# A third Strassen level over pairs of steps, in three of seven rounds of a float32 linear layer

## The chip, the cores and the metric

The kernel runs on one core of a Trainium2 chip. The metric is the device time of one execution in microseconds (us), as the median of several runs. TensorE (PE) multiplies; VectorE (DVE) adds products from the accumulation banks (PSUM) into partial sums in SBUF; GpSimd (POOL) makes sums and differences of operands in SBUF; SyncE (SP) issues most of the loads and stores.

## The reference

All arrays are float32. The part that matters here is the first feed-forward layer, a linear map over the last axis of length 2048, applied to `x` of shape (32, 128, 2048):

```
out = einsum('bsd,od->bso', x, W) + bias                  # W is 2048 x 2048
upd = sum over e of coeffs[e]*scales[e] * (x A_e^T) Bf_e^T  # 16 updates of rank 16
x   = x + out + upd    # after a mixing of the 128 rows, per batch entry
```

In the kernel the low-rank updates are first added to `W`, so that one product with a 2048 x 2048 matrix is left. The mixing of the rows (`agg_w`, 128 x 128 for each batch entry) commutes with that product and is done after it. Then follow a grouped convolution with 9 taps along the length and a second feed-forward layer with 16 heads (128 to 512 to 128, with a gelu), whose rows are permuted.

## The kernel before

The linear layer is done with Strassen's scheme in Winograd's form, on two levels.

The **outer level** splits `x` and the weights into two by two blocks and gives seven products, the *rounds*, in the order `ROUNDS = ("P1", "P2", "P6", "P7", "P5", "P3", "P4")` (line 48). The two row blocks are the two halves of a group of four batch entries. A round needs one sum or difference of weight blocks and, for each of eight groups `g`, one sum or difference of x blocks. A *step* is one round and one group, `(r, g)`; there are 56, numbered `i`.

The **inner level** is in `multiply` (line 322). For a step it makes seven products, again called P1 to P7, each of four matmuls over chunks `kc` of 128 of the contraction, with an x tile of 128x128 as the stationary operand and a weight tile of 128x512 as the moving one. Three PSUM banks (`px`, `py`, `pz`) hold running sums of these products, and after every product `add` has DVE add the bank into one 128x512 part of a partial sum in SBUF. The partial sums of a round are loaded from DRAM (`olds_load`, line 908), added to, and stored again under a new name (`ADDED`, line 312; `part_store`, line 268). Round P5 has two partials per step, the others have one.

The operands are made on POOL. `x_combine` (line 288) makes the block of x of the outer level (`pieces`, line 271, 4 operations for each sum of two tiles) and then the four inner sums `s` (lines 302 to 305). `inner_weights` (line 238) makes the inner weights `t1`, `t2`, `t4` (12 operations) and one difference in place (4 operations), once per round, in the last step of the round before (in round P1, in its seventh step). `outer_weights` (line 369) loads the weight blocks of the next round during steps g = 2 to 5 of this one, one chunk `kc` in a step, and its `combine` adds them in the step after: P6 has three source tiles per chunk, P7 and P5 two, P4 two, P3 one.

Order: the program is scheduled by hand (`tc.manual_schedule()`), so that each engine and each queue works in the order of the code. In step `i` the code issues `x_combine` for step `i+1`, the x loads for step `i+2`, the load of the partial of step `i+1`, at the last step of a round `inner_weights` for the next, then the combination of a weight chunk and the load of the next one, then the matmuls of step `i`, and at their end the store of the partial, which stands on SP's queue ahead of the loads of the next step.

Most tiles are slots of one pool `big` of 24 (`SLOTS = 24`, line 35), each 128 x 2048 float32. A new tile takes the place of one whose last reader or writer is done; where no slot is free, the instruction that writes the new tile first waits, and with it all behind it on its queue.

Three other things use slots or engines in these rounds. `mixed_kernel` (line 402) puts small DVE operations between the products of the first six steps of a round (`between`) and holds one slot. The generator `small` (line 727) goes on by one piece after each step; in round P2 it makes the transformed convolution weights in two slots, `tw` and `t1` (lines 832 to 855). The convolution in the last part of the kernel has the only other matmuls with 256 columns (`conv_product`, line 539).

Of the kernel before, what the change touches and what calls it, by code (L numbers as in the profile page):

```python
# [11 lines left out]
ALU = mybir.AluOpType  # L12
# [4 lines left out]
P = 128  # L17
# [10 lines left out]
NQ = QW // 2  # L28
# [19 lines left out]
ROUNDS = ("P1", "P2", "P6", "P7", "P5", "P3", "P4")  # L48


@with_exitstack
def adaln_ffn_kernel(
    ctx: ExitStack,
# [15 lines left out]
    nc = tc.nc  # L69
# [8 lines left out]
    def slot(name, shape=(P, L)):  # L78
        return big.tile(list(shape), FP, name=name, tag="s")


    def bank():
        return banks.pop(0)

    def done(*ps):
        banks.extend(ps)

    def scratch(name, shape=(P, L)):
        return dram.tile(list(shape), FP, name=name, tag=name)
# [178 lines left out]
    def part_store(n, g, t, eng=nc.gpsimd):  # L268
        eng.dma_start(part_d[n, g], t.rearrange("p k s c -> p (k s c)"))

    def pieces(out, a, b, op):

        for i in range(2):
            for j in range(2):
                nc.gpsimd.tensor_tensor(out[:, i, j], a[:, i, j], b[:, i, j], op)  # L275
# [12 lines left out]
    def x_combine(r, g, ts):  # L288

        a = ts[0]  # L290
        tt = nc.gpsimd.tensor_tensor
        if r == "P6":

            b, a, c = ts
            pieces(b, b, a, ALU.add)
            pieces(a, b, c, ALU.subtract)
            part_store("s2", g, a)
        if r in ("P7", "P5", "P3"):
            pieces(a, a, ts[1], ALU.add if r == "P5" else ALU.subtract)
        s = slot(f"s_{r}{g}", (P, 4, QW))  # L300
        a11, a12, a21, a22 = a[:, 0, 0], a[:, 1, 0], a[:, 0, 1], a[:, 1, 1]
        tt(s[:, 0], a21, a22, ALU.add)  # L302
        tt(s[:, 1], s[:, 0], a11, ALU.subtract)
        tt(s[:, 2], a11, a21, ALU.subtract)
        tt(s[:, 3], a12, s[:, 1], ALU.subtract)
        return {
            "P1": a11, "P2": a12, "P3": s[:, 3], "P4": a22,
            "P5": s[:, 0], "P6": s[:, 1], "P7": s[:, 2],
        }


    ADDED = {
        "P1": [(None, "p1")],
        "P2": [("p1", "c00")],
        "P6": [("p1", "u1")],
        "P7": [("u1", "u2")],
        "P5": [("u1", "u3"), ("u2", "c11")],
        "P4": [("u2", "c10")],
        "P3": [("u3", "c01")],
    }  # L320

    def multiply(r, g, lhs, rhs, olds, between):
        px, py, pz = bank(), bank(), bank()
        accs = olds if olds[0] is not None else [slot(f"m_{r}{g}", (P, 2, 2, QW))]
        fresh = set()

        def add(si, oi, ps):
            for acc in accs:
                to = acc[:, si, oi]
                if olds[0] is not None or (si, oi) in fresh:  # L330
                    nc.vector.tensor_tensor(to, ps, to, ALU.add)  # L331
                else:
                    nc.scalar.copy(to, ps)
            fresh.add((si, oi))

        def product(k, ps, first, last):
            for kc in range(4):
                nc.tensor.matmul(  # L338
                    ps, lhsT=lhs[k][:, bass.ts(kc, P)], rhs=rhs[k][kc],
                    start=first and kc == 0, stop=last and kc == 3, skip_group_check=True,  # L340
                )

        product("P1", px, True, False)
        add(0, 0, px)
        between(0)
        product("P2", pz, True, True)
        add(0, 0, pz)
        done(pz)
        between(1)
        product("P6", px, False, False)  # L350
        add(0, 1, px)
        between(2)
        product("P5", py, True, False)
        add(1, 1, py)
        between(3)
        product("P7", px, False, False)
        add(1, 1, px)
        between(4)
        product("P3", py, False, True)
        add(0, 1, py)  # L360
        done(py)
        between(5)
        product("P4", px, False, True)
        add(1, 0, px)
        done(px)
        for (_, new), acc in zip(ADDED[r], accs):
            part_store(new, g, acc, nc.sync)

    def outer_weights(r, kc):

# [129 lines left out]
    def conv_inputs(c, i, part):  # L500
# [27 lines left out]
        else:  # L528
# [3 lines left out]
            w0, w5 = v0[:, :, 1:NM], v5[:, :, 0 : NM - 1]  # L532
            stt(w0, d[3][:, :, 0 : NM - 1], 4.0, w0, ALU.mult, ALU.add)
            stt(w5, d[0][:, :, 1:NM], 0.25, w5, ALU.mult, ALU.add)

    def halves(t):
        return [t[:, r * NQ : (r + 1) * NQ] for r in range(2)]

    def conv_product(ps, k, i, v, first, last):

# [321 lines left out]
    steps = [(r, g) for r in ROUNDS for g in range(NG)]  # L862
# [19 lines left out]
    lhs, sa, tb = {}, {}, {}  # L882
    sa[0] = a_combine(0, nc.gpsimd.tensor_tensor)
    first = [wt.pop(k) for k in blocks[0:4]]
# [15 lines left out]
    rhs = inner_weights("P1", first, make_first)  # L900
    a_load(1, 0, 4)
    unsummed, unsummed_first = [], list(first)
    olds = {}
    chain = small()
    nxt, waiting, ts = {}, {}, {}
# [6 lines left out]
    for i, (r, g) in enumerate(steps):  # L912
        ri = i // NG
        last_round = ri + 1 == len(ROUNDS)
        if i + 1 < len(steps):
            if i + 1 not in xs:
                xs[i + 1] = x_loads(*steps[i + 1])
            if not last_round:
                lhs[i + 1] = x_combine(*steps[i + 1], xs.pop(i + 1))
        if i + 2 < len(steps) and ri > 0 and not last_round:  # L920
            xs[i + 2] = x_loads(*steps[i + 2])
        if i == 0:
            olds_load(0)
        if i + 1 < len(steps) and not last_round:
            olds_load(i + 1)
        if g == NG - (1 if ri else 2) and ri < len(ROUNDS) - 1:
            nxt = inner_weights(ROUNDS[ri + 1], [nxt[kc] for kc in range(4)])

        if ri == 0:
            ks = blocks[4 + 2 * g : 6 + 2 * g]  # L930
            if ks:
                two = [wt.pop(k) for k in ks]
                w_make_two(ks, two, sa[ks[0][0]], tb[ks[0][1]])
                made.extend(ks)
                if g == 1:
                    a_scale(1, 0, 4)
                    sa[1] = a_combine(1, nc.gpsimd.tensor_tensor)
                if g == 3:
                    part, tb[0] = b_combine(0, nc.gpsimd.tensor_tensor)
                    for _ in range(4):  # L940
                        part()
                for k, t in zip(ks, two):
                    unsummed.append((k[1], t))
                    if k[:2] == (1, 0):
                        nxt[k[2]] = t
        elif ri + 1 < len(ROUNDS):
            for k, combine in waiting.items():
                nxt[k] = combine()
            waiting = {}
            if 2 <= g < 6:  # L950
                waiting[g - 2] = outer_weights(ROUNDS[ri + 1], g - 2)

        if last_round and g == 0:
            late_loads()
        if last_round and g == 2:

            late["te"] = mix.rearrange("p (k r) c -> p k r c", k=2)
            nc.sync.dma_start(mix.rearrange("p k c -> p (k c)"), te_d)
        k0 = 3 * (g - NG)
        if last_round:  # L960
            stage(k0, stage_first)

        def between(j):
            b = (ri - 1) * (NG - 2) + g
            if ri > 0 and g < NG - 2 and b < B and j < KEXP // 2:
                mixed_kernel(b, (2 * j, 2 * j + 1))
            if ri == 0 and j == 2:
                for k in blocks[6 + 2 * g : 8 + 2 * g]:
                    wt[k] = w_load(*k)
            if ri == 0 and j in (1, 3) and unsummed:  # L970
                row_sums(*unsummed.pop())
            if ri == 0 and j == 5 and unsummed_first:
                t = unsummed_first.pop(0)
                tt = nc.vector.tensor_tensor
                tt(wsum[:, 0, 0], wsum[:, 0, 0], t[:, 0, 0], ALU.add)
                tt(wsum[:, 0], wsum[:, 0], t[:, 1], ALU.add)
            if last_round:
                if j == 3 and i + 1 < len(steps):
                    lhs[i + 1] = x_combine(*steps[i + 1], xs.pop(i + 1))
                    olds_load(i + 1)  # L980
                if j in (2, 4):
                    stage(k0 + j // 2, stage_first)
                if j % 2:
                    stage_third(k0 + j // 2)
                else:
                    stage(k0 + j // 2, stage_second)

        multiply(r, g, lhs.pop(i), rhs, olds.pop(i), between)
        next(chain, None)
        if last_round and g >= 6:  # L990
            pair(g - 6)
        if last_round and g == 7:
            rings()
            gather_two(0)
        if g == NG - 1 and ri + 1 < len(ROUNDS):
            rhs = nxt
            nxt = {}

    before = None
    for k, (g, h) in enumerate(heads):  # L1000
# [5 lines left out]
        t = ts.pop(k)  # L1006
# [75 lines left out]
```

## Time and profile before

| | |
|---|---|
| median of 3 runs | 2629.42 us (2627.97 to 2631.45) |
| the profiled execution | 2628.45 us |
| its span, first to last instruction | 2626.7 us |
| granted TensorE clock, mean | 0.999 |
| PE busy | 2611.2 us, 99% |
| POOL busy | 1234.8 us, 47% |
| DVE busy | 1349.3 us, 51% |
| HBM traffic | 372.45 MB read, 200.84 MB written |

In a list of groups a row gives the line, engine, operation and tile names, the count, the busy time and the mean duration of one. In a timeline a row gives the start, the time from the start of the first to the end of the last, what it is, and in brackets how long the engine was idle before it and for whom it waited. In a table of stretches each row gives the stretch, its length, the busy time of PE, PEld (the load of stationary operands), DVE, ACT and POOL with the count of instructions, the granted clock, the share of DMA and the rate in GB/s. A float32 matmul appears as two instructions of PE, called passes here, each with a load of the stationary operand before it. PE's rows overlap their successors, so passes are compared from start to start.

### The profile page before, as it was taken

What the parts mean: (1) busy time and instruction counts of PE and PEld (TensorE: products, weight loads), DVE (VectorE), ACT (ScalarE), POOL (GpSimd) and SP (SyncE); (2) the same over time, 40 slices, a digit from 0 to 9 for tenths busy, and PEclk for the clock granted to TensorE, in tenths of its full rate; (3) what the DMA queues carried; (4) which work ended last, traced back from release to release, by engine and by line L of the source; (5) the groups of instructions that cost most, each with busy time, mean ns of one, the idle gap of its engine ahead of it and who ended that gap; (6) DMA issues with size and microseconds to landing.
All of it is one profiled execution on the core that took longest, in us unless ns stands there. A gap on an engine that the chain in (4) does not pass through costs nothing.

```text
span 2626.7 us, 20239 instructions
## 1 busy us (share of the span) xinstructions
PE 2611.2 (99%) x6468; PEld 1228.9 (47%) x6468; DVE 1349.3 (51%) x2178; ACT 532.9 (20%) x1099; POOL 1234.8 (47%) x1014
## 2 busy tenths in 40 slices
PE   9999999999999999999999999999999999999998
PEld 4444444444444444444444445555444555555543
DVE  5554234354233454433366666666666666666610
ACT  0000000000000000000011144444444444444432
POOL 7320636888756644756342334434443344344222
PEclk9999999999999999999999999999999999999999
DMA  7542358688466577565668798777778777777532
GB/s 304 223 162 109 130 222 310 270 338 351 159 241 256 221 285 294 224 243 202 224 221 256 223 319 284 234 228 220 225 249 250 243 225 222 238 250 232 166 121 88
DMA packets 183833, 608.20 MB, mean 232 GB/s; under 512 B 17200, under 2 KB 88368, under 8 KB 139440
## 3 DMA queue, kind: packets, MB, share of 16 engines
q1 hardware_dynamic: 149936, 473.74, 50.8%
q0 software_dynamic: 32992, 132.14, 14.9%
q10 hardware_dynamic: 800, 1.03, 0.1%
q8 instruction: 52, 0.85, 0.1%
q14 instruction: 53, 0.43, 0.1%
HBM read 372.45 MB, written 200.84 MB: 218 GB/s over the span
## 4 chain that ended last, share of the span: by engine, by line
PE 98%; DVE 1%; DMA 1%; issue 0%; SPq 0%; POOLq 0%; ACT 0%; DVEq 0%; ACTq 0%
PE bank L338 51%; PE bank L687 16%; PE bank L698 16%; PE bank L543 6%; PE bank L448 4%; PE bank L216 3%; PE bank L173 1%; DMA ws<-in_ffw 0%; DVE vb L523 0%; DVE va L522 0%; DMA bf_sb<-in_BfT 0%; DVE vb L521 0%; DVE va L524 0%; DMA out<-t,orow 0%; DVE aggb L782 0%
## 5 line engine op out<-in xcount | busy, mean ns | idle before, releaser
L687 PE MATMUL bank<-t,ws 128*128 128x512 f32 x1024 | 460.4, 592 | 0.8 <-DMA ws<-in_ffw 0.8
L698 PE MATMUL bank<-gl,ws 128*128 128x512 f32 x1024 | 460.2, 592 | 0.0
L705 POOL DMA_INDIRECT out<-t,orow x128 | 153.5, 1199 | 532.2 <-DVE t L703 451.6
L331 DVE TENSOR_TENSOR u<-bank,u 128x512 f32<-128x512 f32 x280 | 187.9, 688 | 416.5 <-PE bank L338 409.4
L690 ACT ACTIVATE gl<-bank 128x512 f32<-128x512 f32 x512 | 306.2, 598 | 446.2 <-PE bank L687 443.2
L338 PE MATMUL bank<-P_t,s_P 128*128 128x512 f32 x896 | 393.7, 592 | 0.0
L698 PEld LDWEIGHTS bank<-gl,ws 128*128 128x128 f32 x1024 | 194.6, 190 | 233.0 <-issue 231.0
L687 PEld LDWEIGHTS bank<-t,ws 128*128 128x128 f32 x1024 | 194.5, 190 | 227.7 <-issue 223.6
L433 POOL TENSOR_TENSOR x<-x,fb 128x512 f32<-128x512 f32 x128 | 178.0, 1418 | 228.1 <-DMA x<-in_x 201.0
L338 PE MATMUL bank<-wo_P,s_P 128*128 128x512 f32 x640 | 281.6, 592 | 0.9 <-DVE u L331 0.9
L338 PE MATMUL bank<-wo_P,xt 128*128 128x512 f32 x640 | 281.5, 592 | 0.0
L338 PEld LDWEIGHTS bank<-P_t,s_P 128*128 128x128 f32 x896 | 170.2, 190 | 213.4 <-issue 211.2
L703 DVE TENSOR_TENSOR t<-bank,t 128x512 f32<-128x512 f32 x128 | 88.5, 691 | 316.1 <-PE bank L698 315.9
L439 ACT ACTIVATE bank<-w,aggb 128x512 f32<-128x512 f32 x128 | 80.8, 683 | 793.6 <-DMA w<-w_d 776.3
L275 POOL TENSOR_TENSOR xt<-xt,xt 128x512 f32<-128x512 f32 x128 | 160.0, 1283 | 150.3 <-DMA xt<-in_xT 135.5
L338 PE MATMUL bank<-P_t,xt 128*128 128x512 f32 x448 | 201.4, 592 | 0.0
L331 DVE TENSOR_TENSOR p<-bank,p 128x512 f32<-128x512 f32 x112 | 77.5, 692 | 228.5 <-PE bank L338 225.1
L338 PEld LDWEIGHTS bank<-wo_P,s_P 128*128 128x128 f32 x640 | 121.5, 190 | 153.0 <-issue 149.7
L338 PEld LDWEIGHTS bank<-wo_P,xt 128*128 128x128 f32 x640 | 121.6, 190 | 152.2 <-issue 150.9
L302 POOL TENSOR_TENSOR s_P<-xt 128x512 f32<-128x512 f32 x56 | 72.3, 1291 | 254.8 <-DMA xt<-in_xT 198.0
L412 DVE SCALAR_TENSOR_TENSOR ags<-mix,att_bc,ags 128x128 f32<-128x128 f32 x224 | 162.9, 727 | 4.5
L671 POOL DMA_INDIRECT t<-hx_d,row x128 | 131.9, 1030 | 50.6 <-issue 26.0
(141 smaller groups left out, 2648.9 us busy)
## 6 DMA issues: line engine op xcount, KB each, us to landing
xt<-in_xT SPq DMA_DIRECT2D x88, 1024.0 KB, 9.0
u<-u_d SPq DMA_DIRECT2D x40, 1024.0 KB, 11.0
wo_P<-wb_d SPq DMA_DIRECT2D x36, 1024.0 KB, 14.4
u<-c_d SPq DMA_DIRECT2D x64, 512.0 KB, 7.3
x<-in_x SPq DMA_DIRECT2D x32, 1024.0 KB, 8.0
xg<-x SPq DMA_DIRECT2D x256, 128.0 KB, 5.1
hx_d<-x1t SPq DMA_DIRECT2D x32, 1024.0 KB, 6.0
hx_d<-ht SPq DMA_DIRECT2D x32, 1024.0 KB, 7.1
```

Source lines behind the costliest of these rows:

```text
L275: nc.gpsimd.tensor_tensor(out[:, i, j], a[:, i, j], b[:, i, j], op)
L331: nc.vector.tensor_tensor(to, ps, to, ALU.add)
L338: nc.tensor.matmul(ps, lhsT=lhs[k][:, bass.ts(kc, P)], rhs=rhs[k][kc], start=first and kc == 0, stop=last and kc == 3, skip_group_check=True,)
L412: nc.vector.scalar_tensor_tensor(ag, mix[:, k], att, ag, ALU.mult, ALU.add)
L433: nc.gpsimd.tensor_tensor(xt[:, f], xt[:, f], late["fb"][:, f], ALU.add)
L448: nc.tensor.matmul(pm, lhsT=ag, rhs=u[:, f], start=False, stop=True, skip_group_check=True)
L543: nc.tensor.matmul(out, lhsT=w[:, 2 * i + r], rhs=rhs, start=first and r == 0, stop=last and r == 1, skip_group_check=True,)
L671: nc.gpsimd.indirect_dma_start(out=t.rearrange("p k t -> p (k t)"), out_offset=None, in_=hx_d[g].rearrange("l k t -> l (k t)"), in_offset= ...
L687: nc.tensor.matmul(pu, lhsT=w[:, m * P : (m + 1) * P], rhs=t[:, 0], start=True, stop=True)
L690: nc.scalar.activation(gl[m], pu, AF.Gelu)
L698: nc.tensor.matmul(pd, lhsT=w[:, (MC + m) * P : (MC + m + 1) * P], rhs=gl[m], start=(m == 0), stop=(m == MC - 1),)
L705: nc.gpsimd.indirect_dma_start(out=out, out_offset=bass.IndirectOffsetOnAxis(ap=orow[:, g, h : h + 1], axis=0), in_=t[:, 1], in_offset=None,)
```

## The change

In rounds P2, P7 and P3 the inner products P2 and P4 of two neighbouring steps (an even `g` and the next) are taken together. The two steps give two blocks of rows, the contraction is cut into two halves of 256 and the columns into two halves of 256, and each of the two inner products is made by seven products of a third Strassen level, *quarters*. A quarter is made for both inner products at once, in the two halves of one PSUM bank: for each, two matmuls of 128x128 by 128x256.

- `multiply_third` takes the place of `multiply` in these rounds. In an even step it makes five products (P1, P5, P6, P3, P7). In the odd step it makes these five and the seven quarters, in three more banks (`qx`, `qy`, `qz`), and DVE adds each quarter's bank into one half of a partial of one of the two steps. The bank after product P7 is added into two parts of the partial, where P4's was added into the second before. Both partials are stored at the end of the odd step.
- `third_inputs` makes four sums of x blocks per pair on POOL, into one slot, right after the `x_combine` of the odd step. `third_weights` makes eight differences for each of the two inner products on POOL (16 operations of 128x256, two slots), right after `inner_weights`, so in the last step of the round before (for P2, in the seventh step of P1).
- The x tile of the even step and its partial stay in their slots until the odd step uses them.

```diff
+THIRD = ("P2", "P7", "P3")
...
+    def third_weights(name, rhs):
+        quarters, tt = [], nc.gpsimd.tensor_tensor
+        for i, k in enumerate(("P2", "P4")):
+            t = slot(f"{name}_q{i}", (P, 4, 2, NQ))
...
+            for kc in range(2):
+                (r11, r12), (r21, r22) = (halves(rhs[k][2 * h + kc]) for h in range(2))
+                tt(t[:, 0, kc], r12, r11, ALU.subtract)
+                tt(t[:, 1, kc], r22, t[:, 0, kc], ALU.subtract)
+                tt(t[:, 2, kc], r22, r12, ALU.subtract)
+                tt(t[:, 3, kc], r21, t[:, 1, kc], ALU.subtract)
...
+    def third_inputs(i):
+        (x11, x12), (x21, x22) = (
+            [xa[n][:, 1, :, h * NQ : (h + 1) * NQ] for h in range(2)] for n in (i, i + 1)
+        )
...
+        t = slot(f"sq_{i}", (P, 4, 2, NQ))
+        tt(t[:, 0], x21, x22, ALU.add)
+        tt(t[:, 1], t[:, 0], x11, ALU.subtract)
+        tt(t[:, 2], x11, x21, ALU.subtract)
+        tt(t[:, 3], x12, t[:, 1], ALU.subtract)
...
+    def multiply_third(r, g, lhs, rhs, olds, between, quarters, sq):
+        px, py = bank(), bank()
+        if sq:
+            qx, qy, qz = bank(), bank(), bank()
+            both = [held.pop(), olds]
...
+        def quarter(k, ps, first, last, *to):
+            if not sq:
+                return
+            for i, out in enumerate(halves(ps)):
+                for kc in range(2):
+                    nc.tensor.matmul(
+                        out, lhsT=sq[k][:, i, bass.ts(kc, P)], rhs=quarters[i][k][kc],
...
+            for b, h in to:
+                for acc in both[b]:
+                    part = acc[:, :, 0, h * NQ : (h + 1) * NQ]
+                    nc.vector.tensor_tensor(
+                        part, ps.rearrange("p (s n) -> p s n", s=2), part, ALU.add
+                    )
+        product("P1", px, True, False)
+        add(0, 0, px)
+        between(0)
+        quarter("P1", qx if sq else None, True, False, (0, 0))
+        quarter("P2", qz if sq else None, True, True, (0, 0))
...
+        product("P5", py, True, False)
+        add(1, 1, py)
+        between(1)
+        quarter("P6", qx if sq else None, False, False, (0, 1))
+        quarter("P5", qy if sq else None, True, False, (1, 1))
+        product("P6", px, False, False)
+        add(0, 1, px)
+        between(2)
+        quarter("P7", qx if sq else None, False, False, (1, 1))
+        quarter("P3", qy if sq else None, False, True, (0, 1))
...
+        product("P3", py, False, True)
+        add(0, 1, py)
...
+        quarter("P4", qx if sq else None, False, True, (1, 0))
...
+        product("P7", px, False, True)
+        add(1, 1, px)
+        add(1, 0, px)
...
+        if not sq:
+            held.append(olds)
+            return
+        for b, accs in enumerate(both):
+            for (_, new), acc in zip(ADDED[r], accs):
+                part_store(new, g - 1 + b, acc, nc.sync)
...
@@ the loop over the steps
                 lhs[i + 1] = x_combine(*steps[i + 1], xs.pop(i + 1))
+                if r in THIRD and g % 2 == 0:
+                    sq = third_inputs(i)
...
             nxt = inner_weights(ROUNDS[ri + 1], [nxt[kc] for kc in range(4)])
+            if ROUNDS[ri + 1] in THIRD:
+                nxt["quarters"] = third_weights(ROUNDS[ri + 1], nxt)
...
-        multiply(r, g, lhs.pop(i), rhs, olds.pop(i), between)
+        if r in THIRD:
+            multiply_third(
+                r, g, lhs.pop(i), rhs, olds.pop(i), between, rhs["quarters"], sq if g % 2 else None
+            )
+        else:
+            multiply(r, g, lhs.pop(i), rhs, olds.pop(i), between)
```

More of the change, by code (lines that the diff above doesn't have):

```diff
@@ L86, in done, with halves @@
         banks.extend(ps)
+    def halves(t):
+        return [t[:, r * NQ : (r + 1) * NQ] for r in range(2)]
     def scratch(name, shape=(P, L)):
@@ L299, in x_combine @@
             pieces(a, a, ts[1], ALU.add if r == "P5" else ALU.subtract)
+        xa[steps.index((r, g))] = a
         s = slot(f"s_{r}{g}", (P, 4, QW))
@@ L309, in x_combine @@
         }
+    xa = {}
     ADDED = {
@@ L367, in multiply @@
             part_store(new, g, acc, nc.sync)
+    def third_weights(name, rhs):
+        quarters, tt = [], nc.gpsimd.tensor_tensor
+        for i, k in enumerate(("P2", "P4")):
+            t = slot(f"{name}_q{i}", (P, 4, 2, NQ))
+            q = {"P1": [], "P2": [], "P3": [], "P4": [], "P5": [], "P6": [], "P7": []}
+            for kc in range(2):
[4 more added lines that the diff above has]
+                tt(t[:, 3, kc], r21, t[:, 1, kc], ALU.subtract)
+                for n, r in zip(q, (r11, r21, r22, t[:, 3, kc], t[:, 0, kc], t[:, 1, kc], t[:, 2, kc])):
+                    q[n].append(r)
+            quarters.append(q)
+        return quarters
@@ new lines, in third_inputs @@
+    def third_inputs(i):
+        (x11, x12), (x21, x22) = (
+            [xa[n][:, 1, :, h * NQ : (h + 1) * NQ] for h in range(2)] for n in (i, i + 1)
+        )
+        tt = nc.gpsimd.tensor_tensor
+        t = slot(f"sq_{i}", (P, 4, 2, NQ))
[3 more added lines that the diff above has]
+        tt(t[:, 3], x12, t[:, 1], ALU.subtract)
+        return {
+            "P1": x11, "P2": x12, "P3": t[:, 3], "P4": x22,
+            "P5": t[:, 0], "P6": t[:, 1], "P7": t[:, 2],
+        }
@@ new lines, in multiply_third, with add, product @@
+    def multiply_third(r, g, lhs, rhs, olds, between, quarters, sq):
[3 more added lines that the diff above has]
+            both = [held.pop(), olds]
+        def add(si, oi, ps):
+            for acc in olds:
+                nc.vector.tensor_tensor(acc[:, si, oi], ps, acc[:, si, oi], ALU.add)
+        def product(k, ps, first, last):
+            for kc in range(4):
+                nc.tensor.matmul(
+                    ps, lhsT=lhs[k][:, bass.ts(kc, P)], rhs=rhs[k][kc],
+                    start=first and kc == 0, stop=last and kc == 3, skip_group_check=True,
+                )
[4 more added lines that the diff above has]
+                for kc in range(2):
+                    nc.tensor.matmul(
+                        out, lhsT=sq[k][:, i, bass.ts(kc, P)], rhs=quarters[i][k][kc],
+                        start=first and i == 0 and kc == 0, stop=last and i == 1 and kc == 1,
+                        skip_group_check=True,
+                    )
[4 more added lines that the diff above has]
+                        part, ps.rearrange("p (s n) -> p s n", s=2), part, ALU.add
+                    )
+        product("P1", px, True, False)
[3 more added lines that the diff above has]
+        quarter("P2", qz if sq else None, True, True, (0, 0))
+        if sq:
+            done(qz)
+        product("P5", py, True, False)
[8 more added lines that the diff above has]
+        quarter("P3", qy if sq else None, False, True, (0, 1))
+        if sq:
+            done(qy)
+        product("P3", py, False, True)
+        add(0, 1, py)
+        done(py)
+        between(3)
+        quarter("P4", qx if sq else None, False, True, (1, 0))
+        if sq:
+            done(qx)
+        product("P7", px, False, True)
+        add(1, 1, px)
+        add(1, 0, px)
+        done(px)
+        between(4)
+        between(5)
+        if not sq:
[4 more added lines that the diff above has]
+                part_store(new, g - 1 + b, acc, nc.sync)
@@ L369, in outer_weights @@
+    held = []
     def outer_weights(r, kc):
@@ L534, in conv_inputs @@
             stt(w5, d[0][:, :, 1:NM], 0.25, w5, ALU.mult, ALU.add)
-    def halves(t):
-        return [t[:, r * NQ : (r + 1) * NQ] for r in range(2)]
     def conv_product(ps, k, i, v, first, last):
@@ L986, in between @@
                     stage(k0 + j // 2, stage_second)
-        multiply(r, g, lhs.pop(i), rhs, olds.pop(i), between)
+        if r in THIRD:
+            multiply_third(
+                r, g, lhs.pop(i), rhs, olds.pop(i), between, rhs["quarters"], sq if g % 2 else None
+            )
+        else:
+            multiply(r, g, lhs.pop(i), rhs, olds.pop(i), between)
+        xa.pop(i - 1, None)
         next(chain, None)
```

## The prediction

> **What bounds the kernel now.** I read the page first: busy times, slices, chain. TensorE is busy in every slice at full granted clock, and the chain that ended last is 98% PE.
>
> ```profile
> PE 2611.2 (99%) x6468; PEld 1228.9 (47%) x6468; DVE 1349.3 (51%) x2178; ACT 532.9 (20%) x1099; POOL 1234.8 (47%) x1014
> ...
> PEclk9999999999999999999999999999999999999999
> ...
> PE 98%; DVE 1%; DMA 1%; issue 0%; SPq 0%; POOLq 0%; ACT 0%; DVEq 0%; ACTq 0%
> ```
>
> So only removed matmul time helps, and only while PE keeps being fed. Next, the seven rounds as stretches (P2 begins at 306.5 us, each step lasts 24.03, the chain's "24.03 PE bank L338 x56").[...]
>
> ```profile
> 306.50:498.70 192.20, 192.20 (x449) 85.05 (x449) 73.18 (x109) 2.37 (x4) 106.38 (x87) 1.00 0.67 256
> 498.70:691.00 192.30, 192.30 (x450) 85.15 (x449) 83.80 (x106) 0.63 (x1) 172.66 (x143) 1.00 0.76 298
> 691.00:883.20 192.20, 192.20 (x450) 85.05 (x449) 68.47 (x104) 0.00 (x0) 114.58 (x94) 1.00 0.59 229
> ```
>
> P2, P6, P7 (P3 is like P7): PE never idles, POOL has 70 to 86 of 192 us left in the rounds that change. Third, the timeline of PE around a convolution, the only 256-column matmuls, and of POOL and SP at the end of round P2:
>
> ```profile
> 1341.46 1.88 PE L338 MATMUL bank<-wo_P,s_P 128*128 128x512 f32 x4
> 1343.18 1.89 PE L543 MATMUL bank<-va,tw_l 128*128 128x256 f32 x8
> 1344.91 3.60 PE L338 MATMUL bank<-P_t,xt 128*128 128x512 f32 x8
> ```
> ```profile
> 480.89 1.27 POOL L245 TENSOR_TENSOR P_t<-wo_P 128x512 f32<-128x512 f32 x1 [1.77 <-issue]
> 485.16 1.27 POOL L246 TENSOR_TENSOR P_t<-wo_P,P_t 128x512 f32<-128x512 f32 x1 [2.99 <-PE bank L338]
> 488.59 1.27 POOL L247 TENSOR_TENSOR P_t<-wo_P,P_t 128x512 f32<-128x512 f32 x1 [2.17 <-PE bank L338]
> ```
> ```profile
> 451.44 0.32 SPq L269 DMA_DIRECT2D c_d<-p  x1
> 451.86 4.78 SPq L260 DMA_DIRECT2D xt<-in_xT  x3
> 456.73 0.38 SPq L265 DMA_DIRECT2D p<-p_d  x1
> ```
>
> [...]Four passes of 512 columns start 1.72 us apart (0.429 each), eight of 256 take 1.73 (0.216 each). The other two say that the 24 slots of SBUF are already used up at the end of P2: POOL waits for PE to finish with the old weights before t2 and t4 of P6 have a place (474.7+10.3 and +13.7 us are the ends of that round's last P6 and P5 products), and three loads take 4.78 us to issue because the third waits for a freed source tile. Counting live tiles through the code gives exactly 24 at that point, so the count can be trusted.
>
> **The change, part by part.**
>
> *PE.* Per pair of steps the P2 and P4 products go: 2 steps x 2 products x 4 chunks x 2 passes = 32 passes x 0.429 = 13.73 us. They are replaced by 7 quarters x 4 matmuls x 2 passes = 56 passes x 0.216 = 12.10. Saved: 1.63 a pair; three rounds of four pairs make 12 pairs, **19.5 us**. All of it lies on the path. An even step becomes 5 x 3.43 = 17.2 us long, an odd one 17.2+12.1 = 29.3.
>
> A rule speaks against this. The Trainium skill, "TensorE: Matmul & The Clock Gate", section "The mechanism", says that a weight load overlaps a running matmul only when it goes to another row group. All matmuls here use all 128 rows, and a load lasts 190 ns in the groups; by the rule a pair would go from 32 x (0.429+0.19) = 19.8 to 56 x (0.216+0.19) = 22.7, which is 35 us slower over 12 pairs. The rows above show 0.216 from start to start with a load before each pass, so the loads are hidden, and I take the rows. The cover is thin: 190 of 216 ns.
>
> *DVE.* Additions into one partial: 14 a pair before; now 6 in each step and 7 after quarters, 19. 5 x 0.69 = 3.5 us a pair, 41 in all, beside PE: DVE has 68 to 73 us busy of 192 here and needs 19 x 0.69 + 16 x 0.74 (mixed_kernel) = 25 of 46 us a pair. Between a quarter and the next use of its bank lie at least 5 us of PE. Nothing, while the partials are there in time.
>
> *POOL.* third_inputs: 4 operations of the size of s (1.27 us), 5.1 a pair. P7 rises from 114.6 to 135 us of about 186. third_weights: 16 operations of 128x256, a size that the trace lacks. Half of 1.27 is the lower end (10 us), 1.27 the upper (20). POOL's memsets (225 ns for 128 columns, 1794 for 2048) have a fixed part of some 0.12 us, so I take 0.69, 11 us. They stand before the next x_combine. For P6 to P7 that POOL queue would finish inner_weights at 685.2, third_weights at 696.3, and the first x piece at 697.6, needed at 691+17.2 = 708.2: hidden. For P5 to P3: 1077.7+11.1+1.3 = 1090.1, needed at 1092.7: hidden by 2.6 us only. P1 to P2 has the sum for P5 ready at 304.5, wanted at 309.9. At the upper end the last two cost about 10 us together.
>
> *Queues.* SP's loads are those of before. Even steps have no store, odd ones two, so at the odd step SP issues loads a step earlier, if there are slots. A store stands behind the next weights' loads; if one of these waits, the two stores wait, and with them the two slots of the finished partials.
>
> *Slots.* This is the price. Live for a whole changed round: +2 (quarter weights). In an odd step also sq, the even step's input and its partial: +5 in all. At the end of P7 the count was 24 and of P3 22; there the surplus tiles are the next round's weights and partials, which get slots as the old weights die (10.3 and 17.2 us into the last step) and at its quarter P4 (25.8), 3.4 us before the next round. POOL makes P5's t2 in 11 operations x 1.3 = 14.3 us from there, 40.1; P6's fourth chunk wants it at 38.7. Up to 1.5 us for P7, none for P3.
>
> P2 is worse: tw and t1 of the convolution (2 slots) live in its second half, and P6 wants three source tiles per weight chunk and three x tiles. At step 14 (even): weights 9, ags 1, tw and t1 2, P6's chunks 3 with 3 sources, input, sums, partial and next input 4: 22. s for step 15 and the first x of step 16 fill 24. Still to be placed, in SP's order, are two more x tiles and the partial of step 15, and on POOL sq. They get: the sums of step 14 at its end (sq), that step's input after quarters P1 and P2 (+6.9 us of step 15), the old t1 after product P5 (+10.3), and a source tile after POOL's sq (5.1) and pieces (5.1), +10.2. So the partial's load is issued near +10.5. PE reaches quarter P6 at +10.3, whose bank waits for an addition on DVE that is queued behind the one into that partial. DMA to landing at this line: "7.5/10.6/16.4". Few transfers are ahead of it, so I take 9, plus two additions (1.4): **10 us of PE idle at step 15**, with 7.5 and 16.4 as its ends 9 and 18. Step 13 has the same shortage, milder: DVE's tw needs a slot that comes 6.9 us into it, 1 us. P6's first partial, issued when quarter P4 frees slots: 1 us.
>
> Sum: -19.5 + 12 = **-7.5 us** on the profiled execution, 2628.45 (span 2626.7 and 1.75 around it): 2621. The median shown is 1 us higher, so 2622.
>
> **The rivals.**
>
> 1. *Slots cost more than the quarters save* (slower). If in P2 the slots of the two stored partials go to s and sq, the x tiles of step 16 wait for step 14's end and step 15's t1, the pieces run later, and the partial's load is issued at +18 instead of +10.5; with 11 us to landing and the additions PE stands for 20 at step 15, 3 at step 14 (its partial lands 2.6 late), 1.5 at P7's end and 1.5 at P6's start: 26, net +6.5, 2636. It decides from 19.5 us of idle PE. For it: POOL's waits at 485 and 488, and that the order in which tiles get slots is written into the program. Against: before, with the same shortage at 451 to 457, PE did not wait once in P2.
>
> 2. *All is hidden*: slots come in time, 2610. For it: no L338 wait over 1 us in the rounds before. Against: the count, 22 slots taken before four tiles ask.
>
> 3. *About even*: step 15 costs 16 and the POOL queue or P7's end 4 more, 2629. For it: the upper ends above.
>
> 4. *Weight loads show in the quarters*, as the rule has it: +35 us. The rows at 1343 speak against it. The change failing to do what it says is not one: the passes are counted from the code.
>
> **How the numbers follow.** A measurement of this kernel can tell about 0.2%, 5.3 us. The likeliest case (7 to 14 us lost) gets 0.40, its own range 2616 to 2624; all hidden 0.10; about even 0.25; slots beyond the saving 0.23; loads shown 0.02. So faster 0.50, same 0.25, slower 0.25. The forecast is the likeliest case's, 2622. The range goes from the full gain, 2610, to just beyond rival 1, 2638; outside lie a few per cent below and about one in ten above.
>
> **What would show it.** Right: PE instructions 6468+288 = 6756; a group of 256-column passes in multiply_third, 672, 0.216 apart; P7 and P3 rounds of about 186 us without PE idle; one PE wait of about 10 us near 306.5+156+10 = 473, released by DVE, and DVE's by the load of a partial (p from p_d). Wrong: quarter passes over 0.24 apart; PE waits on POOL's s or sq in P7 or P3; idle PE in P2 of more than 19 us, or none at all.

## The result, and the profile after

The changed kernel takes 2630.3 us (median of 14 runs), the kernel before 2628.8 on the same chip: ratio 1.0005, 95% interval 0.9997 to 1.0013. No difference that a measurement can tell, where 7 us less were forecast. The page of the profile after, its busy times, the granted clock by slice, and the chain that ended last:

```profile
span 2629.9 us, 20983 instructions
...
PE 2593.0 (99%) x6756; PEld 1283.2 (49%) x6756; DVE 1407.7 (54%) x2238; ACT 532.6 (20%) x1099; POOL 1326.1 (50%) x1110
...
PEclk9999999899999999999999999999999999999999
...
PE 94%; DMA 2%; DVE 2%; POOL 1%; issue 1%; SPq 0%; POOLq 0%; ACT 0%; DVEq 0%; ACTq 0%
```

PE did lose work: 18.2 us of busy time, with the 288 passes more that were counted. But the chain is no longer PE alone: 2% of the span is DMA and 1% POOL, where it was 1% and 0%, and one slice has a clock below full. The rounds as stretches:

```profile
305.80:512.00 206.20, 187.34 (x546) 104.32 (x545) 83.91 (x128) 2.36 (x4) 120.03 (x100) 0.96 0.62 238
512.00:704.80 192.80, 192.49 (x449) 85.00 (x448) 87.60 (x107) 0.63 (x1) 179.47 (x151) 1.00 0.76 298
704.80:890.50 185.70, 185.70 (x546) 103.38 (x545) 87.38 (x123) 0.00 (x0) 135.44 (x114) 1.00 0.61 238
...
1082.80:1268.40 185.60, 185.60 (x545) 103.30 (x544) 87.83 (x124) 0.00 (x0) 142.18 (x122) 1.00 0.56 221
```

Row three is P7 and row four P3: 6.5 and 6.6 us shorter than before, PE busy throughout. Row one is P2: 14.0 us *longer*. All of PE's waits from 230 to 1310 us are these two (who waits, for whom: us in total, how many times, the longest):

```profile
PE bank L435 <- DVE p L443: 18.9, 1, 18.9
PE bank L347 <- POOL P_t L252: 0.3, 1, 0.3
```

So the gain of all three rounds was given back in one place. Here it is on the four engines, PE, DVE, POOL and SP in turn:

```profile
468.97 3.60 PE L424 MATMUL bank<-P_t,s_P 128*128 128x512 f32 x8
491.43 5.07 PE L435 MATMUL bank<-P_q,sq 128*128 128x256 f32 x16 [18.86 <-DVE p L443]
```
```profile
489.99 0.69 DVE L420 TENSOR_TENSOR p<-bank,p 128x512 f32<-128x512 f32 x1 [25.62 <-DMA p<-p_d]
490.60 1.41 DVE L443 TENSOR_TENSOR p<-bank,p 128x512 f32<-128x512 f32 x2
```
```profile
456.20 1.25 POOL L309 TENSOR_TENSOR s_P<-xt 128x512 f32<-128x512 f32 x1 [17.46 <-DVE p L420]
...
461.20 1.27 POOL L402 TENSOR_TENSOR sq<-xt 128x512 f32<-128x512 f32 x1
...
466.68 9.81 POOL L281 TENSOR_TENSOR wo_P<-wo_P,wo_P 128x512 f32<-128x512 f32 x8
```
```profile
445.52 1.23 SPq L275 DMA_DIRECT2D c_d<-p  x2
471.64 5.69 SPq L266 DMA_DIRECT2D xt<-in_xT  x3
477.43 0.39 SPq L271 DMA_DIRECT2D p<-p_d  x1
```

Read it from the bottom. SP issues the two stores of steps 12 and 13 at 445.5 and then nothing for 25 us: its next entry, the first x tile of step 16, wants a slot that holds a source tile of POOL's weight sum. POOL waits too: s of step 15 gets a slot only when the first store has landed, 10.5 us after its issue. (The row names DVE, whose addition ended 0.1 us before; in `p2_only`, below, POOL starts before that addition ends.) Then it works without a gap through s, sq and the weight pieces, until 476.5. The first half of the pieces frees one slot (471.64), the second half the next (three loads take 5.69 us to issue), and only then the partial of step 15 goes out, at 477.43. It lands 12.4 us later; DVE, idle for 25.6 us, adds; and PE, which stood ready for quarter P6 at 472.6, goes on at 491.43. Its next 16 passes take 5.07 us; without the wait, in the run `both` below, they take 3.62.

The stretches around that wait show why:

```profile
465.70:484.60 18.90, 6.86 (x24) 4.18 (x23) 0.00 (x0) 0.00 (x0) 13.27 (x12) 0.80 0.53 178
484.60:505.00 20.40, 13.57 (x45) 9.53 (x46) 6.04 (x9) 0.00 (x0) 14.73 (x13) 0.76 0.79 300
505.00:512.00 7.00, 7.00 (x22) 3.92 (x21) 1.38 (x2) 0.00 (x0) 4.02 (x4) 1.00 0.88 276
```

The granted clock was 0.80 and 0.76 on average in the first two stretches and 1.00 in the third. In shorter stretches it falls to 0.50 at 477.1, 4.5 us into the wait, and is back at 1.00 from 494.2, 2.8 us after PE went on. The wait cost 18.9 us and the slower clock about 1.5 more. With 0.3 at the start of P6 these make 20.6 us, against 19.5 saved. Most of the 3.2 us between the two spans is in the last part of the kernel (2.5 us longer, with the same matmuls). That is spread between executions: in `before_hold3`, below, this part is the code of the kernel before, and it is 2.7 us longer too.

### The profile page after: what moved, and what is told of

Same layout as the page of the kernel before. It is cut to its first block, busy times and chain, and to the rows that moved or that the text cites. A ratio compares the mean times of both kernels' runs of the same rounds, so it can differ in the third digit from the quotient of the medians.

```text
span 2629.9 us, 20983 instructions
## 1 busy us (share of the span) xinstructions
PE 2593.0 (99%) x6756; PEld 1283.2 (49%) x6756; DVE 1407.7 (54%) x2238; ACT 532.6 (20%) x1099; POOL 1326.1 (50%) x1110
## 4 chain that ended last, share of the span: by engine, by line
PE 94%; DMA 2%; DVE 2%; POOL 1%; issue 1%; SPq 0%; POOLq 0%; ACT 0%; DVEq 0%; ACTq 0%
PE bank L347 28%; PE bank L803 16%; PE bank L814 16%; PE bank L424 15%; PE bank L659 6%; PE bank L435 5%; PE bank L567 4%; PE bank L222 2%; DMA bf_sb<-in_BfT 1%; DMA p<-p_d 0%; DVE vb L642 0%; DMA ws<-in_ffw 0%; DVE vb L640 0%; POOL wo_P L281 0%; DVE va L641 0%
## 5 line engine op out<-in xcount | busy, mean ns | idle before, releaser
L340 DVE TENSOR_TENSOR u<-bank,u 128x512 f32<-128x512 f32 x168 | 110.3, 684 | 165.9 <-PE bank L347 163.4
L531 DVE SCALAR_TENSOR_TENSOR ags<-mix,att_bc,ags 128x128 f32<-128x128 f32 x224 | 178.8, 798 | 4.5
L347 PE MATMUL bank<-wo_P,s_P 128*128 128x512 f32 x384 | 169.1, 592 | 0.9 <-DVE u L340 0.9
L347 PE MATMUL bank<-wo_P,xt 128*128 128x512 f32 x384 | 169.0, 592 | 0.0
L347 PEld LDWEIGHTS bank<-P_t,s_P 128*128 128x128 f32 x512 | 97.2, 190 | 122.3 <-issue 118.6
L787 POOL DMA_INDIRECT t<-hx_d,row x128 | 130.9, 1023 | 50.1 <-issue 25.6
L420 DVE TENSOR_TENSOR u<-bank,u 128x512 f32<-128x512 f32 x96 | 64.9, 690 | 167.9 <-PE bank L424 150.2
L659 PE MATMUL bank<-va,tw_l 128*128 128x256 f32 x512 | 122.4, 380 | 1.9 <-DVE va L643 1.8
L659 PEld LDWEIGHTS bank<-va,tw_l 128*128 128x128 f32 x512 | 96.6, 190 | 44.6 <-issue 34.2
```

What stands on the lines that cost most here:

```text
L347: nc.tensor.matmul(ps, lhsT=lhs[k][:, bass.ts(kc, P)], rhs=rhs[k][kc], start=first and kc == 0, stop=last and kc == 3, skip_group_check=True,)
L531: nc.vector.scalar_tensor_tensor(ag, mix[:, k], att, ag, ALU.mult, ALU.add)
L659: nc.tensor.matmul(out, lhsT=w[:, 2 * i + r], rhs=rhs, start=first and r == 0, stop=last and r == 1, skip_group_check=True,)
L787: nc.gpsimd.indirect_dma_start(out=t.rearrange("p k t -> p (k t)"), out_offset=None, in_=hx_d[g].rearrange("l k t -> l (k t)"), in_offset= ...
```

## The experiments

**Theory A**: the loss sits in one place. The 24 slots are short at the end of P2, and with them the partial of step 15 is late. **Rival B**: POOL's queue, which makes four sums more per pair, is late by its own work. **Rival C**: the third level costs something in every round.

**Without P2** (`no_p2`).

```diff
-THIRD = ("P2", "P7", "P3")
+THIRD = ("P7", "P3")
```

> The third level in rounds P7 and P3 only; P2 as before. Theory A (the whole loss sits in one place, step 15 of round P2, where a partial is loaded late for want of a slot): both rounds keep their 6.5 us each, nothing else is lost, about 2628.8 - 13 = 2616 us. Rival C (part of the loss belongs to the third level in every round, spread over the rest of the run): less than 10 us gained, 2619 or more.

Measured 2616.9 us against 2628.7, ratio 0.9954 (0.9941 to 0.9968), and no wait of PE in the rounds. 11.9 us gained, nearly the 13 of theory A. P7 and P3 take 185.7 us each, as in the changed kernel.

**P2 alone** (`p2_only`).

```diff
-THIRD = ("P2", "P7", "P3")
+THIRD = ("P2",)
```

> The third level in round P2 only. Theory A: P2's 6.5 us of saved matmuls against 18.9 of waiting and 1.6 of slower passes after it: 2628.8 + 14 = 2643 us, and the sum of this change and of P7 and P3 alone gives the whole change. Rival C (the loss comes from the three rounds together): less than 5 us lost.

Measured 2643.1 against 2629.0, ratio 1.0054 (1.0040 to 1.0068): 14.1 us lost, as A has it, with one wait of 18.8 us at the same place (PE's row names POOL's x pieces there, but DVE's next row again waits 25.7 us for the partial, and PE goes on after its additions). The two parts, -11.9 and +14.1, add to +2.2; the whole change measured +1.5. Rival C is out.

**Only the slots** (`before_hold3`): the kernel before, with three slots held.

```diff
         multiply(r, g, lhs.pop(i), rhs, olds.pop(i), between)
+        if i == 11:
+            hold = [slot(f"hold{k}") for k in range(3)]
+            for t in hold:
+                nc.vector.memset(t[:, 0:8], 0.0)
+        if i == 15:
+            for t in hold:
+                nc.vector.memset(t[:, 0:8], 0.0)
```

> The kernel before, without any third level; three slots of the 24 are only held from step 11 to step 15 of round P2 (a memset of 8 columns at each end). Theory A (slots): the x tiles of step 16 now stand on POOL's source tiles, as in the changed kernel, the partial of step 15 behind them is issued at about the start of step 15 (474.7 us) instead of 456.7 and lands 8 to 11 us later, where it is wanted at 481; PE waits 1 to 4 us there and as much at the start of P6: 2630 to 2637 us. Rival B (the work of the third level on POOL and DVE, not the slots): no change, 2628.8.

Measured 2642.9, ratio 1.0051 (1.0038 to 1.0065): 13.9 us lost with no third level at all and no work beyond six tiny memsets. PE, SP and POOL of this kernel at that place:

```profile
475.03 7.03 PE L338 MATMUL bank<-w,xt 128*128 128x512 f32 x16
493.29 9.59 PE L338 MATMUL bank<-P_t,s_P 128*128 128x512 f32 x16 [11.23 <-DVE p L331]
```
```profile
451.92 0.32 SPq L269 DMA_DIRECT2D c_d<-p  x1
473.63 6.17 SPq L260 DMA_DIRECT2D xt<-in_xT  x3
479.90 0.39 SPq L265 DMA_DIRECT2D p<-p_d  x1
```
```profile
463.67 1.25 POOL L302 TENSOR_TENSOR s_P<-xt 128x512 f32<-128x512 f32 x1 [20.17 <-DMA c_d<-p]
```

It is the same picture: POOL waits until a store has landed before it can make s, SP is silent for 21 us after a store, three x tiles take 6 us to issue because of POOL's source tiles, the partial behind them goes out at 479.9 instead of 456.7, PE is idle for 11.2 us and its next 16 passes take 2.6 us longer. So a shortage of slots is enough by itself, and rival B is not needed. In the changed kernel the four sums sq, 5.5 us of POOL's work, also stand ahead of the weight pieces; what share of the 18.9 us is theirs, no run separates. My size was too small: I had the partial issued at 475 and no slower clock.

**The partial ahead of the x loads** (`olds_first`).

```diff
-        if i + 2 < len(steps) and ri > 0 and not last_round:
-            xs[i + 2] = x_loads(*steps[i + 2])
         if i == 0:
             olds_load(0)
         if i + 1 < len(steps) and not last_round:
             olds_load(i + 1)
+        if i + 2 < len(steps) and ri > 0 and not last_round:
+            xs[i + 2] = x_loads(*steps[i + 2])
```

> All three rounds; in each step the load of the next step's partial is put on SP's queue ahead of the x loads of the step after. The slots are as short as in the changed kernel. Theory A: the partial of step 15 takes the slot of the first source tile that POOL frees (471.6 us in the changed kernel's trace) instead of standing behind three x tiles until 477.4, and lands 7.5 to 10.6 us later: PE idle there 8 to 12 us instead of 18.9, and round P6 may start 1 to 5 us late because its x tiles come later; 2621 to 2626 us. Rival B (POOL's queue, with s, sq and the weight pieces one after the other, is what is late, whatever the order of the loads): idle time as before, 2630.

Measured 2628.6, ratio 1.0001 (0.9993 to 1.0009): no net gain, where 3 to 8 us had been expected. The wait moved. PE at the old place and at the start of P6:

```profile
478.37 5.72 PE L435 MATMUL bank<-P_q,sq 128*128 128x256 f32 x16 [5.39 <-DVE p L443]
...
507.52 1.12 PE L347 MATMUL bank<-P_t,s_P 128*128 128x512 f32 x2 [1.08 <-POOL P_t L252]
511.47 2.08 PE L347 MATMUL bank<-P_t,s_P 128*128 128x512 f32 x2 [2.83 <-POOL P_t L252]
515.38 2.07 PE L347 MATMUL bank<-P_t,s_P 128*128 128x512 f32 x2 [1.83 <-POOL P_t L252]
519.27 6.62 PE L347 MATMUL bank<-P_t,s_P 128*128 128x512 f32 x10 [1.83 <-POOL P_t L252]
```

The partial does come earlier, and the wait falls from 18.9 to 5.4 us, so the order on SP's queue was part of the cause. But the x tiles of step 16 now come later, POOL waits 10.4 us for them and makes the weights of P6 late: four waits, 7.6 us together, and the clock falls a second time (mean 0.74 from 499 to 526 us). By starts of rounds P2 is still 7.6 us over its 185.7, and P6 is now 12.6 over 192.3. The slots are as short as before; whoever is served first, another is late.

**Two slots more** (`late_tw`): the convolution weights are made 22 steps later.

```diff
+        for _ in range(22):
+            yield
+
         tw, t1 = slot("tw", (P, 4, GR, P)), slot("t1", (P, 4, GR, P))
```

> All three rounds; the transformed convolution weights are made 22 steps later, in round P5, so that two slots are free in the second half of P2. The order of the loads is that of the changed kernel. Theory A: s of step 15 and sq no longer wait for stores, but the partial still stands behind an x tile that waits for POOL's second source tile: idle 4 to 12 us at step 15; 2615 to 2624. Rival B: POOL's own work is the same, but starts earlier, the same sign; this run alone doesn't part A from B.

Measured 2612.6, ratio 0.9937 (0.9924 to 0.9951). The wait at step 15 is 3.0 us, s of step 15 starts at 442.4 instead of 456.2, the partial is issued at 464.2 instead of 477.4. Two slots are worth 17.7 us here, 2630.3 against 2612.6 (the loads and the DVE operations of these weights move with them); 4.2 us less than that, 2608.4, is what the next run reaches.

**Both edits** (`both`).

> Both edits: partial ahead of the x loads, convolution weights 22 steps later. Theory A: the partial of step 15 gets the slot of step 13's sums, is loaded before step 14 begins, and PE does not stop: all of the 19.4 us, 2609 to 2612. Rival B: POOL still makes s, sq and the pieces in a row before the x tiles of step 16, and PE would wait at the end of P2 or the start of P6: 2616 or more.

Measured **2608.4**, ratio 0.9923 (0.9910 to 0.9937): 20.3 us less than before, the whole of what the quarters save, and faster than either kernel. PE's only wait in the rounds, and its row at the old place:

```profile
PE bank L435 <- POOL sq L403: 0.5, 1, 0.5
```
```profile
472.37 3.62 PE L435 MATMUL bank<-P_q,sq 128*128 128x256 f32 x16
```

P2 takes 185.7 us here. POOL does the same work as in the changed kernel, s, sq and pieces one after the other, from 441.7 to 462.9 instead of from 456.2 to 476.5. That speaks once more against rival B: it was not POOL's work but the wait ahead of it.

**How far it goes.** Two runs put the third level into a fourth round. `p5_tw6` adds P5, with the partial ahead of the x loads and the convolution weights only 6 steps later, so that their two slots are taken in P6. `both_p6` is `both` with P6 added.

> Partial ahead of the x loads; the convolution weights made 6 steps later, in round P6; the third level in P5 as well. P5 has two partials per step, so an odd step holds six more slots than before, and the count at P5's end is full before four tiles of the next round are placed. Theory A: of 6.5 us more to gain (2602 if all comes) 5 to 20 are given back by waits at the end of P5 or in its odd steps: 2607 to 2620. Rival (slots are no longer short once the partial is ahead of the x loads): 2602.

> Both edits, and the third level in P6 as well. P6 has POOL busy for 173 of 192 us; third_inputs adds 20 and third_weights for P7 is 11 more, while PE would need 186. POOL would set the round: 195 to 205 us, so 2610 to 2620. If slots alone decide, as far as POOL goes nothing is lost: 2602 to 2606.

With P5 too: 2625.8, ratio 0.9988 (0.9979 to 0.9996). With P6 too: 2635.1, ratio 1.0023 (1.0014 to 1.0031). Both lose more than I expected, 17 and 27 us against `both`, and in both PE waits for pieces of x, not for a partial; first P5, then P6:

```profile
PE bank L424 <- POOL xt L281: 15.7, 2, 9.0
```
```profile
PE bank L424 <- POOL xt L281: 23.6, 3, 13.9
```

For P6 POOL is the bound, as foreseen, but in one place and not over the round: it works without a gap from 484 to 537 (inner weights, quarter weights, x pieces and more), PE waits 13.9 us for the pieces at the second step and then runs through to the end of P6. The next long wait, 9.1 us, stands in the same way at the second step of P7. For P5 the two waits stand at the second step of P5 and of P3, where the 11.5 us of quarter weights and the x pieces stand one behind the other on POOL and the even step, with 17.2 us, gives them less time than 24.0. In P3 of the changed kernel that is hidden by 2.0 us (the first piece ends at 1097.7, PE wants it at 1099.8); the third level in P5 used that up, and slots in P5 were short too (SP waited there for PE and POOL to free them). How the 15.7 us divide between the two no run shows.

## Why the prediction was right or wrong

- *PE's saving*, 19.5 us: right. P7 and P3 are 6.5 and 6.6 us shorter, and quarter passes stand 0.216 apart (16 in 3.45 us in P7). Weight loads of 190 ns stay hidden behind passes of 216. So the sentence that spoke against it (the Trainium skill, "TensorE: Matmul & The Clock Gate", section "The mechanism") does not hold in this kernel. The same section also lets a load be pulled ahead when it goes to a background weight buffer; whether that is the way here, no run shows.
- *DVE and POOL beside PE*: right. third_weights' operations take 0.72 us (0.69 predicted), P7 has POOL busy for 135.4 us (135), and PE waits for nothing at the start of P2, P7 or P3. The changed kernel has no wait at step 13, where 1 us had been put, and none at P7's end, where up to 1.5 were allowed for; P6's start costs 0.3 instead of 1.
- *The slots at step 15*: the place, the engine and the chain were right (PE at quarter P6, held by DVE's queue, held by the load of a partial; at 472.6, where 473 was written), the size was not. The failing term is "10 us of PE idle at step 15": it was 18.9, and 1.5 more from the clock. Three things were mis-sized. The partial was issued 15.4 us into step 15 (which began at 462.1), not 10.5: s got the slot of a stored partial, as in rival 1, so POOL's pieces ran later, and the first x tile took the slot of one of their source tiles and held SP's queue until 471.6, while I had given it a slot that came free earlier. The landing took 12.4 us, not 9: I took few transfers to be ahead of it, and SP's three x loads were released just before it. And a slower clock after the wait was not in the sum.
- *What that makes*: 20.6 us of loss against 19.5 saved. The forecast of a gain failed; the range held only because it was wide enough for the rivals. The time is rival 3's (2629), but not by its account, which had 16 us at step 15 and 4 at POOL's queue or P7's end. Rival 1 was nearer in mechanism and in size at step 15 (20 us), and put 6 us more at places where next to nothing was lost. The line "22 slots taken before four tiles ask" was the important one; how the program deals out these slots decides between 10 and 20 us, and the count alone did not give it.

## What to carry to other kernels

When PE is the bound and everything else is hidden, ask what the change keeps alive longer. Three rounds gained the same; one lost three times as much (20.4 against 6.5 us), because five tiles more met a pool that was already full there, with a load that PE needs queued behind loads that it does not need yet. Count live tiles at the worst step, not on average, and look at what else is parked there: moving two unrelated tiles to another round and one load ahead of others turned no gain into 20 us.

## What the runs showed of the hardware

- A wait of PE costs more than its length, but what it costs afterwards did not grow with it. From the first start to the last end, 16 passes after 18.9 us of idling took 5.07 us instead of 3.62, after 5.4 us (`olds_first`) 5.72, and after 3.0 us (`late_tw`) 3.69; after 11.2 us (`before_hold3`) 16 wider ones took 9.59 instead of 7.03. So 1.5, 2.1, 0.1 and 2.6 us more.
- In the changed kernel, `olds_first` and `before_hold3` the granted clock fell to 0.50, in that order 4.5, 2.7 and 2.6 us after PE had run dry, and came back 2.8, 4.1 and 5.0 us after it went on; in `late_tw` it stayed at 1.00. These runs give no limit below which a wait is safe: in `olds_first` the clock fell again at 509.8, in the second of two waits of 1.1 and 2.8 us, each shorter than the one in `late_tw`.
- A float32 matmul of 256 columns costs half of one of 512, with a new stationary operand for every matmul: 0.216 against 0.429 us per pass, in the 672 passes of the changed kernel but for those after the wait.
